# Image rows of the second 13x13 convolution in seven tiles instead of four, and the large kernels merged in the first scan

## The chip, the cores and the metric

The kernel runs on one core of a Trainium2 chip. It is one launch that computes a whole four-layer network. The metric is the time of the core on the device in microseconds (us); a lower time is better. Times of a kernel are medians of several runs. Profiles come from one profiled execution, whose own time stands beside its span.

## The reference

Input and output are x[8, 384, 32, 32] in fp32: 8 images (B), 384 channels (C), 32 x 32 pixels. Four layers follow each other:

```
layer 0: xn = rmsnorm(x);  x += res_scale * (scale_mod * (mamba(xn) + flip(mamba(flip(xn))))
                                             + sigmoid(dwconv3x3(xn)) * xn)
layer 1: conv mixer (1x1, depthwise 3x3, 1x1), linear attention, then an MLP with GELU, each residual
layer 2: out = sum over 7 depthwise kernels (13x13, 5x5, 7x7, 7x7 dil. 2, 3x3 dil. 3, 4, 5),
               each with its own batch norm
layer 3: x_pw = bn(einsum('bchw,oc->bohw', x, pw_w)) + x
         out  = gelu(bn(dwconv13x13(x_pw)) + bn(x_pw * dw1_w))
```

The mamba of layer 0 holds a recurrence over the 1024 pixels of an image, h = dA * h + dBu, for 384 channels x 16 states, once forward and once backward. As convolutions are linear, the seven kernels of layer 2 can be added up into one 13x13 kernel per channel, and the two branches of layer 3 into another.

## The kernel before

**Scans.** Image by image (8 scans, one per image), `scan(b)` runs the recurrence in 12 units (direction, half image, 128 channels) of 4 rounds. A round has two half-rounds of this kind: ScalarE makes `da` (L840), VectorE multiplies `du` (L845), runs two scan instructions (L857) and in half of the units saves a `carry` (L862), GpSimd multiplies the result `hs` by C (L866), and TensorE sums it into `acc` (L551). The inputs `dlt`, `vr` (L786) and `bct` (L772) are loaded by SP, one unit ahead. Eight `hs` tiles are in turn.

**What is woven into the scans.** `jobs` (L1189) is a list of generators with a total cost and a stretch of rounds in which each is due; after every round the loop lets the job that is furthest behind yield once. There are `fold()` (layer 1's weights scaled), `prepare` (below), `front(b)` for the next image and `layer1(b)` for the one before. Tiles called `w` (four in turn, `wtile`, L511) hold weights for all of these, and the merged kernels too. The framework then schedules the instructions: the built order of an engine can differ from that of the program's text.

**Merging the large kernels.** `kernels(small, large)`, run as the job `prepare`, makes for each of three chunks of 128 channels the merged kernel `g2` of layer 2 and `g3` of layer 3. For each: SP loads the weights (L197, L213), GpSimd clears a `w` tile (L199, L215), VectorE adds each branch scaled into it (`merge`, L184 for the first branch, L186 for the others: 21 instructions for `g2`, 4 for `g3` and one addition, L222), and GpSimd's queue stores it to DRAM (L210, L224). They are read again only at the end of the kernel.

**The two 13x13 convolutions.** After the last scan and the last `layer1`, `conv` runs with `g2` (tag a), then the 1x1 product of layer 3 (L372), then `conv` with `g3` (tag b). `conv` works on 48 tiles of 8 channels. A tile n has

- image rows `xt`: a DMA from DRAM on GpSimd's queue (L296) into 32 partitions, then two VectorE copies (`shift`, L302) that put shifted versions into the other partitions. Four `xt` tiles are in turn.
- a window set `tp`: the merged kernel laid out as bands, four DMAs, two on SP and two on ACT (L245). Twenty are in turn; 16 sets for b are asked for during the product.

Then two groups of 32 matmuls (L326) make four channels each. In b each group ends with a GELU on ScalarE (L394) and a DMA of the result on GpSimd's queue (L395). Six `ot` tiles and six PSUM tiles are in turn. In a, results are copied to `yt` (L340, L342) and stored every four groups (L344).

The order in `conv`: rows of tiles 0 and 1 are loaded, tile 0 is shifted; at the start of tile n, tile n+2 is loaded and n+1 shifted. In the built program, POOL has the loads 0 to 3, then outputs of tile 0, load 4, outputs of tiles 1 and 2, load 5, and from there on always the two outputs of tile n and then load n+3. ACT has the GELUs of tile n and the two DMAs for window set n+20 by turns, up to set 47.

Two pools hold the tiles: `cw` (three `xo` tiles, into which the product writes its rows; its weights `pwt`; `gbias`) and `cx` (`xt`, `yt`, `yp`, `tm`, `ot`). Both stay open to the end.

Of the kernel before, what the change touches and what calls it, by code (L numbers as in the profile page):

```python
# [10 lines left out]
FP = mybir.dt.float32  # L11
# [5 lines left out]
P = 128  # L17
C = 384
NC = C // P
# [21 lines left out]
N_WIN, NCH = 20, 8  # L41
# [27 lines left out]
def tile_layers(  # L69
# [31 lines left out]
    BW = B * W  # L101
# [7 lines left out]
    RL = PADW + B * (W + PADW) + 3  # L109
    x2_d = dram.tile([C, H, RL], FP, tag="x2_d", name="x2_d")  # L110
    y2_d = dram.tile([C, H, B, W], FP, tag="y2_d", name="y2_d")
    xp_d = dram.tile([C, H, RL], FP, tag="xp_d", name="xp_d")
    g2_d = dram.tile([C, NSH, TG, KT], FP, tag="g2_d", name="g2_d")
    g3_d = dram.tile([C, NSH, TG, KT], FP, tag="g3_d", name="g3_d")
# [33 lines left out]
    def bns(name, c):  # L148
        i = _BN.index(name)
        return bn_s[:, c, i : i + 1]  # L150

    def bnt(name, c):
        i = _BN.index(name)
        return bn_t[:, c, i : i + 1]
# [102 lines left out]

    NQ = C // 4
    GB = 4
    with tc.tile_pool(name="cw", bufs=1, reuse_waits="tile") as cwp, tc.tile_pool(  # L260
        name="cx", bufs=2, reuse_waits="tile"
    ) as cxp, tc.tile_pool(
        name="cps", bufs=6, space=PSUM, reuse_waits="tile"
    ) as cps:
        xos = []
        for i in range(3):
            t = cwp.tile([P, NC, 2, RL], FP, tag=f"xo{i}", name=f"xo{i}")
            nc.gpsimd.memset(t, 0.0)
            xos.append(t)
        pwt = cwp.tile([P, NC, C], FP, tag="pwt", name="pwt")  # L270
        nc.scalar.dma_start(pwt, pw_t.rearrange("(k p) o -> p k o", p=P))
        gbias = cwp.tile([P, NQ], FP, tag="gbias", name="gbias")
        for q in range(4):
            nc.scalar.dma_start(gbias[q * H : (q + 1) * H, :], biasq_d[q, :].partition_broadcast(H))
        def conv(g_d, src_d, tag, put):

            xts = {}

            def places(n):

                return [H * ((n % 2 * 2 + e) % NSH) for e in range(NSH)]

            def load(n):
                for m in range(n, min(n + 1 + N_WIN // 2, NB_C)):
                    if (tag, m) not in wins:
                        load_windows(g_d, tag, m, [nc.sync, nc.scalar])
                if n >= NB_C:
                    return  # L290
                at = places(n)
                xt = cxp.tile([P, NCH, RL], FP, tag="xt", name=f"xt_{tag}_{n}", bufs=4)
                src = bass.AP(
                    src_d.tensor, src_d[NCH * n, 0, 0].offset, [[RL, H], [H * RL, NCH], [1, RL]],
                )
                nc.gpsimd.dma_start(xt[at[0] : at[0] + H], src)  # L296
                xts[n] = xt

            def shift(n):
                at, xt = places(n), xts[n]  # L300
                for e in (1, 2):
                    nc.vector.tensor_copy(  # L302
                        xt[at[e] : at[e] + e * H, :, 0 : RL - e - (e - 1)],
                        xt[at[0] : at[0] + e * H, :, e : RL - (e - 1)],
                    )


            for n in range(2):
                load(n)
            shift(0)  # L310
            for g in range(NQ):
                n, first = divmod(4 * g, NCH)
                if first == 0:
                    load(n + 2)
                    if n + 1 < NB_C:
                        shift(n + 1)
                    xt, tp = xts.pop(n), wins[tag, n]
                ps = cps.tile([P, HALF], FP, tag="cv", name=f"cv_{tag}_{g}")
                for t in range(KT):
                    for e in range(4):  # L320
                        c = first + e
                        row = xt[:, c, NSH * t : NSH * t + B * (W + PADW) - PADW]
                        rhs = bass.AP(
                            row.tensor, row.offset, [row.ap[0], [W + PADW, B], [1, W]]
                        )
                        nc.tensor.matmul(  # L326
                            ps[H * e : H * (e + 1), 0:BW],
                            tp[:, c, :].rearrange("p (j t) -> p j t", t=KT)[:, :, t], rhs,
                            start=(t == 0), stop=(t == KT - 1), skip_group_check=True,
                        )  # L330
                put(g, ps[:, 0:BW])

        y2v = y2_d.rearrange("(g q) h b w -> g (q h) (b w)", q=4)
        hold = {}

        def put2(g, ps):
            if g % GB == 0:
                hold["t"] = cxp.tile([P, GB, BW], FP, tag="yt", name=f"yt_{g}")
            if g % 2:
                nc.scalar.copy(hold["t"][:, g % GB, :], ps)  # L340
            else:
                nc.vector.tensor_copy(hold["t"][:, g % GB, :], ps)  # L342
            if g % GB == GB - 1:
                nc.gpsimd.dma_start(y2v[g - GB + 1 : g + 1].rearrange("g p n -> p g n"), hold["t"])  # L344

        conv(g2_d, x2_d, "a", put2)


        pbias = cwp.tile([P, NC, 1], FP, tag="pbias", name="pbias")
        for m in range(NC):  # L350
            ps = cps.tile([P, HALF], FP, tag="cv", name=f"pb_{m}")
            for k in range(NC):
                nc.tensor.matmul(
                    ps[:, 0:1], pwt[:, k, m * P : (m + 1) * P], bias2[:, k, :],
                    start=(k == 0), stop=(k == NC - 1),
                )
            nc.vector.scalar_tensor_tensor(
                pbias[:, m, :], ps[:, 0:1], bns("pw", m), bnt("pw", m), ALU.mult, ALU.add
            )
            nc.vector.tensor_add(pbias[:, m, :], pbias[:, m, :], bias2[:, m, :])  # L360

        yf = y2_d.rearrange("(k p) h b w -> p k (h b w)", p=P)
        xf = xp_d.rearrange("(k p) h r -> p k h r", p=P)
        NB = 2 * BW
        for t in range(H // 2):
            yt = cxp.tile([P, NC, NB], FP, tag="yp", name=f"yp_{t}", bufs=3)
            nc.sync.dma_start(yt, yf[:, :, t * NB : (t + 1) * NB])
            xo = xos[t % 3]
            for m in range(NC):
                ps = cps.tile([P, HALF], FP, tag="cv", name=f"pw_{t}_{m}")  # L370
                for k in range(NC):
                    nc.tensor.matmul(  # L372
                        ps[:, 0:NB], pwt[:, k, m * P : (m + 1) * P], yt[:, k, :],
                        start=(k == 0), stop=(k == NC - 1),
                    )
                tm = cxp.tile([P, NB], FP, tag="tm", name=f"tm_{t}_{m}", bufs=3)
                nc.scalar.activation(  # L377
                    tm, ps[:, 0:NB], AF.Identity, bias=pbias[:, m, :], scale=bns("pw", m)
                )
                for r in range(2):  # L380
                    mid = xo[:, m, r, PADW : PADW + B * (W + PADW)].rearrange("p (b w) -> p b w", w=W + PADW)[:, :, 0:W]
                    nc.vector.tensor_add(  # L382
                        mid, tm[:, r * BW : (r + 1) * BW].rearrange("p (b w) -> p b w", w=W),
                        yt[:, m, r * BW : (r + 1) * BW].rearrange("p (b w) -> p b w", w=W),
                    )
            nc.gpsimd.dma_start(xf[:, :, 2 * t : 2 * t + 2, :], xo)
            if t < N_WIN:
                load_windows(g3_d, "b", t, [nc.scalar, nc.sync])

        ov = out.rearrange("b c h w -> (c h) b w")  # L390

        def put3(g, ps):
            ot = cxp.tile([P, BW], FP, tag="ot", name=f"ot_{g}", bufs=6)
            nc.scalar.activation(ot, ps, AF.Gelu, bias=gbias[:, g : g + 1])  # L394
            nc.gpsimd.dma_start(  # L395
                ov[g * P : (g + 1) * P], ot.rearrange("p (b w) -> p b w", w=W)
            )

        conv(g3_d, xp_d, "b", put3)


def _layers01(tc, nc, B, xv, x2_d, dram, ident, mean_w, eps5, eps6, one, half, minus1, vec, bns, bnt,
# [12 lines left out]
    with ExitStack() as ctx:  # L415
# [7 lines left out]
        def scratch(shape, name):  # L423
            return dram.tile(shape, FP, tag=name, name=name)
# [9 lines left out]
        g_d = scratch([B, C, L], "g_d")  # L434
# [494 lines left out]
        prepare = kernels(t2, lambda name: sp.tile([P, NC * C], FP, tag="w", name=name, bufs=N_W))  # L929
# [254 lines left out]
        rounds = 4 * NC * NR  # L1184
        seconds = [layer1(b) for b in range(B)]


        jobs = [[fold(), 36, 0, rounds, 0], [prepare, 7, rounds, 2 * rounds, 0]]
        for b in range(1, B):  # L1189
            jobs.append([front(b), 100, max(0, (b - 1) * rounds - 8), b * rounds - 8 - 1, 0])  # L1190
        for b in range(B - 1):
# [121 lines left out]
```

## Time and profile before

| what | us |
|---|---|
| median of 3 runs (5093.32 to 5104.8) | 5100.76 |
| the profiled execution's own time | 5049.81 |
| its span | 5048.0 |
| scan of image 0 (142.4 to 668.5) | 526.1 |
| scan of image 1 (671.9 to 1169.6) | 497.7 |
| scan of image 2 (1171.0 to 1663.8) | 492.8 |
| first 13x13 convolution, matmuls (4433 to 4645) | 212 |
| product of layer 3, matmuls (4656 to 4781) | 125 |
| second 13x13 convolution, matmuls (4795 to 5042) | 247 |

Busy over the whole span: TensorE (PE) 83%, VectorE (DVE) 75%, GpSimd (POOL) 59%, ScalarE (ACT) 52%; the mean granted TensorE clock is 0.906.

How to read it. A line of instructions names the line of the program, the engine, the operation, the tiles (out<-in), shapes and the number of instructions. In the list of groups "| busy us, mean ns | idle before us <-releasers" follow. In the timeline, start and duration stand first, and idle time before with what ended it stands in brackets. PEld are weight loads of TensorE; POOLq, SPq and ACTq the issue of an engine's instructions. A row of stretches gives: start and end, length, then busy time and number of instructions for PE, PEld, DVE, ACT and POOL, the granted clock, the share of the 16 DMA engines, and GB/s. The share can exceed 1, as packets in flight overlap.

### The profile page before, as it was taken

Reading aid. Unit: us, or ns where it says so; the run is one execution under the profiler, and the core shown is the slowest. Engines: PE = TensorE matmul, PEld = TensorE weight load, DVE = VectorE, ACT = ScalarE, POOL = GpSimd, SP = SyncE. Lnnn points to the kernel's source line nnn. Section 1 sums busy time; section 2 is a strip of 40 time slices with the busy share of each in tenths; the row PEclk is TensorE's granted clock in tenths of the full one; section 3 lists DMA queues with packets and bytes.
Section 4 is the critical chain, followed back from the end, with each engine's and each line's share of the span. In section 5 each row is a group of like instructions: output and inputs, shape, how many; then the busy total and the mean of one; then the engine's idle time right before and its main releaser. Section 6 shows DMA issues by size and latency. Waiting matters only on the chain. (4 is left out here: it accounts for less than half of the span.)

```text
span 5048.0 us, 58439 instructions
## 1 busy us (share of the span) xinstructions
PE 4205.7 (83%) x20128; PEld 1787.7 (35%) x20128; DVE 3789.3 (75%) x3861; ACT 2632.2 (52%) x3735; POOL 2975.1 (59%) x1546
## 2 busy tenths in 40 slices
PE   7555568898989998988888898988888869978877
PEld 2211113332333333333333333333333324466366
DVE  1689889988988898788978887888898821066256
ACT  3546435784577557756765676568546613100211
POOL 1467567676666676666666666666776750032156
PEclk9676779899989998999899999999898979999989
DMA  8975556577657765776567646765754581399686
GB/s 229 276 235 180 178 157 208 204 219 195 216 181 217 202 215 176 215 207 217 180 199 214 223 170 195 231 211 174 181 169 133 160 177 41 71 215 233 212 189 142
DMA packets 543121, 965.28 MB, mean 191 GB/s; under 512 B 56569, under 2 KB 220905, under 8 KB 542825
## 3 DMA queue, kind: packets, MB, share of 16 engines
q1 hardware_dynamic: 401648, 663.89, 44.2%
q0 software_dynamic: 58048, 205.76, 15.4%
q10 hardware_dynamic: 83128, 91.90, 6.4%
q8 instruction: 159, 2.61, 0.2%
q14 instruction: 138, 1.12, 0.1%
HBM read 726.36 MB, written 234.98 MB: 190 GB/s over the span
## 5 line engine op out<-in xcount | busy, mean ns | idle before, releaser
L866 POOL TENSOR_TENSOR hs<-hs,bct 128x1024 f32<-128x1024 f32 x768 | 2418.2, 3149 | 939.6 <-DVE carry L862 422.9
L840 ACT ACTIVATE da<-dlt,neg_a 128x512 f32<-128x512 f32 x1536 | 1036.7, 715 | 1055.1 <-DVE hs L857 987.9
L857 DVE TENSOR_TENSOR_SCAN hs<-da,carry,du 128x512 f32<-128x512 f32 x768 | 942.7, 1266 | 175.3 <-PE acc L551 129.8
L845 DVE TENSOR_TENSOR du<-vr,bct 128x1024 f32<-128x1024 f32 x768 | 1019.2, 1327 | 46.3 <-DMA vr<-v_d 34.9
L857 DVE TENSOR_TENSOR_SCAN hs<-da,du 128x512 f32<-128x512 f32 x768 | 900.8, 1208 | 128.6 <-PE acc L551 59.9
L551 PE MATMUL acc<-hs,selt 128*32 128x512 f32 x2304 | 546.7, 663 | 140.9 <-POOL hs L866 140.7
L533 PE MATMUL mf<-ln,w 128*128 128x512 f32 x1152 | 546.1, 620 | 22.8 <-DMA w<-w_d 11.7
L1166 PE MATMUL mo<-hm,w 128*128 128x512 f32 x1152 | 530.3, 599 | 13.8 <-DVE xx L1133 13.8
L546 PE MATMUL acc<-hs,selt 128*32 128x512 f32 x768 | 428.5, 653 | 74.4 <-POOL hs L866 63.7
L533 PEld LDWEIGHTS mf<-ln,w 128*128 128x128 f32 x1152 | 222.0, 200 | 331.7 <-issue 270.4
L533 PE MATMUL in<-xn,win 128*128 128x512 f32 x576 | 295.7, 654 | 44.0 <-DMA win<-in_inproj_t 23.6
L1166 PEld LDWEIGHTS mo<-hm,w 128*128 128x128 f32 x1152 | 214.7, 190 | 307.5 <-issue 281.2
L840 ACT ACT_TABLE_LOAD x233 | 298.9, 1283 | 9.5 <-DMA dw_i<-h_d 3.0
L326 PE MATMUL cv_b<-xt_b,tp_b 128*32 128x256 f32 x3072 | 193.6, 407 | 67.9 <-DVE xt_b L302 44.1
L302 DVE COPY xt_b<-xt_b 32x2496 f32<-32x2496 f32 x96 | 147.8, 1540 | 108.0 <-DMA xt_b<-xp_d 103.9
L326 PE MATMUL cv_a<-xt_a,tp_a 128*32 128x256 f32 x3072 | 186.0, 390 | 47.6 <-DVE xt_a L302 21.4
L1136 POOL DMA_DIRECT2D x_d<-xx x48 | 56.5, 1179 | 281.4 <-DVE xx L1133 274.1
L551 PE MATMUL dw<-dw_i,t3b 96*32 96x512 f32 x1056 | 205.6, 656 | 11.1 <-DMA dw_i<-h_d 11.0
L533 PE MATMUL op<-g,wo 128*128 128x512 f32 x288 | 156.4, 695 | 61.3 <-DMA g<-g_d 61.3
L326 PEld LDWEIGHTS cv_b<-xt_b,tp_b 128*32 128x32 f32 x3072 | 163.8, 141 | 98.0 <-issue 69.3
L533 PEld LDWEIGHTS in<-xn,win 128*128 128x128 f32 x576 | 114.1, 207 | 215.2 <-issue 161.5
L326 PEld LDWEIGHTS cv_a<-xt_a,tp_a 128*32 128x32 f32 x3072 | 159.7, 138 | 74.3 <-issue 28.7
(196 smaller groups left out, 5724.7 us busy)
## 6 DMA issues: line engine op xcount, KB each, us to landing
dlt<-dl_d SPq DMA_DIRECT2D x384, 256.0 KB, 4.6
vr<-v_d SPq DMA_DIRECT2D x384, 256.0 KB, 5.0
bct<-bc_d SPq DMA_DIRECT2D x256, 256.0 KB, 3.7
ut<-u_d SPq DMA_DIRECT2D x192, 257.5 KB, 5.5
lc_i<-xn_d SPq DMA_DIRECT2D x192, 228.8 KB, 5.4
dw_i<-h_d SPq DMA_DIRECT2D x192, 228.8 KB, 5.6
w<-w_d SPq DMA_DIRECT2D x64, 576.0 KB, 6.1
w<-in_w SPq DMA_DIRECT2D x64, 576.0 KB, 5.9
```

Of the source, the lines that this page charges most:

```text
L302: nc.vector.tensor_copy(xt[at[e] : at[e] + e * H, :, 0 : RL - e - (e - 1)], xt[at[0] : at[0] + e * H, :, e : RL - (e - 1)],)
L326: nc.tensor.matmul(ps[H * e : H * (e + 1), 0:BW], tp[:, c, :].rearrange("p (j t) -> p j t", t=KT)[:, :, t], rhs, start=(t == 0), stop=(t = ...
L533: product = nc.tensor.matmul(ps, w[:, k, m * P : (m + 1) * P], rhs[k] if isinstance(rhs, list) else rhs[:, k, :], start=(k == 0), stop=(k ...
L546: first = product()
L551: tc.keep_in_program_order(product())
L840: nc.scalar.activation(da[:, bass.ts(j, HALF)], dlt[:, bass.ts(j, HALF)], AF.Exp, scale=neg_a[:, g, r : r + 1],)
L845: nc.vector.tensor_mul(pairs(du), pairs(vt), bct[r][:, 0:1, :].to_broadcast([P, 2, HALF]),)
L857: nc.vector.tensor_tensor_scan(t[:, s][:, way], da[:, s][:, way], du[:, s][:, way], k_c if second else 0.0, ALU.mult, ALU.add,)
L866: made.append(nc.gpsimd.tensor_mul(pairs(t), pairs(t), bct[r][:, 1:2, :].to_broadcast([P, 2, HALF])))
L1136: nc.gpsimd.dma_start(x2v[m, :, h * (H // 2) : (h + 1) * (H // 2), PADW + b * (W + PADW) : PADW + b * (W + PADW) + W,], rows(o),)
L1166: nc.tensor.matmul(acc[m], wb[:, f, m * P : (m + 1) * P], hm, start=(i == 0 and f == 0), stop=(i == FF // C - 1 and f == NC - 1),)
```

## The change

The diff does two things. `conv` gets an argument `far`, how many tiles ahead the rows are loaded: 2 for a as before, 5 for b. For b, tiles n with n % 7 of 4, 5 or 6 come from a new pool `xu` of three, so that seven are in turn. This pool is opened after the pool `cw` is closed, and lies in its place; for that, `cx` is opened first, `gbias` goes to `cx`, and `yt`, `yp`, `tm` go to `cw`. Second, the stretch of the job `prepare` is rounds 0 to 48 (scan of image 0) instead of 48 to 96 (scan of image 1).

```diff
-    with tc.tile_pool(name="cw", bufs=1, reuse_waits="tile") as cwp, tc.tile_pool(
-        name="cx", bufs=2, reuse_waits="tile"
-    ) as cxp, tc.tile_pool(
+    with tc.tile_pool(name="cx", bufs=2, reuse_waits="tile") as cxp, tc.tile_pool(
         name="cps", bufs=6, space=PSUM, reuse_waits="tile"
     ) as cps:
+        gbias = cxp.tile([P, NQ], FP, tag="gbias", name="gbias", bufs=1)
+        mid_ctx = ExitStack()
+        cwp = mid_ctx.enter_context(tc.tile_pool(name="cw", bufs=1, reuse_waits="tile"))
+        more = {}
...
-        def conv(g_d, src_d, tag, put):
+        def conv(g_d, src_d, tag, put, far):
...
-                xt = cxp.tile([P, NCH, RL], FP, tag="xt", name=f"xt_{tag}_{n}", bufs=4)
+                if "pool" in more and n % 7 >= 4:
+                    xt = more["pool"].tile([P, NCH, RL], FP, tag="xu", name=f"xt_{tag}_{n}")
+                else:
+                    xt = cxp.tile([P, NCH, RL], FP, tag="xt", name=f"xt_{tag}_{n}", bufs=4)
...
-            for n in range(2):
+            for n in range(far):
                 load(n)
...
-                    load(n + 2)
+                    load(n + far)
...
-        conv(g2_d, x2_d, "a", put2)
+        conv(g2_d, x2_d, "a", put2, 2)
...
-        conv(g3_d, xp_d, "b", put3)
+        mid_ctx.close()
+        with tc.tile_pool(name="xu", bufs=3, reuse_waits="tile") as more["pool"]:
+            conv(g3_d, xp_d, "b", put3, 5)
...
-        jobs = [[fold(), 36, 0, rounds, 0], [prepare, 7, rounds, 2 * rounds, 0]]
+        jobs = [[fold(), 36, 0, rounds, 0], [prepare, 7, 0, rounds, 0]]
```

In the built program of after, POOL has the loads 0 to 5, the two outputs of tile 0, load 6, and so on: the two outputs of tile n and then load n+6. TensorE's and VectorE's order in both convolutions is unchanged. On VectorE the merges of the first `g2` stand in one block after the `du` of the sixth half-round of scan 0, ahead of image 1's normalisation; those of the second and third `g2` partly singly and partly in a block in the fourth and seventh unit, those of the three `g3` singly in the second, fifth and ninth unit. On SP the loads of some weights (`win_1_1`, `fold_1`) now wait for the store of a merged kernel, whose `w` tile they take over. Outside the scans of images 0 and 1 and the end of the kernel, the order of instructions is as before.

More of the change, by code (lines that the diff above doesn't have):

```diff
@@ L271, in tile_layers @@
         nc.scalar.dma_start(pwt, pw_t.rearrange("(k p) o -> p k o", p=P))
-        gbias = cwp.tile([P, NQ], FP, tag="gbias", name="gbias")
         for q in range(4):
             nc.scalar.dma_start(gbias[q * H : (q + 1) * H, :], biasq_d[q, :].partition_broadcast(H))
-        def conv(g_d, src_d, tag, put):
+        def conv(g_d, src_d, tag, put, far):
             xts = {}
@@ L337, in put2 @@
             if g % GB == 0:
-                hold["t"] = cxp.tile([P, GB, BW], FP, tag="yt", name=f"yt_{g}")
+                hold["t"] = cwp.tile([P, GB, BW], FP, tag="yt", name=f"yt_{g}", bufs=2)
             if g % 2:
@@ L365, in tile_layers @@
         for t in range(H // 2):
-            yt = cxp.tile([P, NC, NB], FP, tag="yp", name=f"yp_{t}", bufs=3)
+            yt = cwp.tile([P, NC, NB], FP, tag="yp", name=f"yp_{t}", bufs=3)
             nc.sync.dma_start(yt, yf[:, :, t * NB : (t + 1) * NB])
@@ L375, in tile_layers @@
                     )
-                tm = cxp.tile([P, NB], FP, tag="tm", name=f"tm_{t}_{m}", bufs=3)
+                tm = cwp.tile([P, NB], FP, tag="tm", name=f"tm_{t}_{m}", bufs=3)
                 nc.scalar.activation(
```

## The prediction

> **What bounds the kernel now.** I read the chain of work that ended last first. Its last 390 us are the product (4656 to 4781 us) and the second 13x13 convolution (4788 to 5044 us), and in the convolution it runs through POOL's DMA issues with idle "issue" stretches of 3.5 to 6 us. Then the groups of that stage:
>
> ```profile
> L326 PE MATMUL cv_b<-xt_b,tp_b 128*32 128x256 f32 x3072 | 193.6, 407 | 67.9 <-DVE xt_b L302 44.1 <-issue 12.5 <-ACT ot L394 11.3
> L395 POOL DMA_DIRECT2D out<-ot x96 | 109.5, 1141 | 98.6 <-ACT ot L394 96.3 <-DVE xt_b L302 1.3 <-issue 0.6
> L302 DVE COPY xt_b<-xt_b 32x2496 f32<-32x2496 f32 x96 | 147.8, 1540 | 108.0 <-DMA xt_b<-xp_d 103.9 <-PE cv_b L326 2.3
> L296 POOL DMA_DIRECT2D xt_b<-xp_d x48 | 48.2, 1004 | 4.7 <-DMA xp_d<-xo 4.4 <-issue 0.3
> ```
>
> TensorE waits for the shifted copies, and VectorE's copies wait 103.9 us for the image rows to land. No engine is full. The timeline shows one such stall:
>
> ```profile
> 4817.47 3.36 DVE L302 COPY xt_b<-xt_b 32x2496 f32<-32x2496 f32 x2 [5.09 <-DMA xt_b<-xp_d]
> 4818.35 1.16 POOL L296 DMA_DIRECT2D xt_b<-xp_d  x1 [0.25 <-issue]
> 4820.94 13.45 PE L326 MATMUL cv_b<-xt_b,tp_b 128*32 128x256 f32 x192 [4.61 <-DVE xt_b L302]
> 4821.35 0.23 PEld L326 LDWEIGHTS cv_b<-xt_b,tp_b 128*32 128x32 f32 x4 [0.20 <-issue]
> 4824.69 0.47 ACT L394 ACTIVATE ot<-cv_b,gbias 128x256 f32<-128x256 f32 x1 [7.78 <-DMA tp_b<-g_d]
> ```
>
> After the gap, weight loads come in fours every 0.43 us until 4826: half speed. At full speed GELUs start 1.81 us apart (4806.11, 4807.91), so a group of 32 matmuls takes 1.81 us and a tile of image rows (two groups) 3.61. The stage runs slower, in two parts: GELUs start at 4798.79 (first), 4949.90 (57th) and 5042.83 (last), which is 5.4 us a tile for the first 28 tiles and 4.65 for the other 20. The first 28 have a window set (the kernel weights of the tile 20 ahead) loading beside them. The stretches, with the first convolution ahead of them for comparison (last columns: granted clock, DMA share, GB/s):
>
> ```profile
> 4433.00:4645.00 212.00, 185.52 (x3070) 159.70 (x3072) 155.88 (x143) 17.51 (x47) 66.09 (x68) 0.98 1.07 244
> 4795.00:4950.00 155.00, 117.99 (x1792) 97.30 (x1792) 85.61 (x56) 26.16 (x56) 88.55 (x81) 0.90 0.92 192
> 4955.00:5044.00 89.00, 71.73 (x1216) 63.15 (x1216) 56.46 (x37) 18.01 (x38) 62.67 (x56) 1.00 0.58 122
> ```
>
> **What the Trainium skill says.** "SBUF — State Buffer", section "SBUF: two separate sides", says that VectorE and GpSimd share a pair of SBUF ports under an exclusive lock, and that GpSimd cannot write DMA descriptors while VectorE copies fp32 in a fast mode. The trace agrees: an output DMA's issue takes 0.89 us at the median but up to 2.16, and ends when a copy of 1.45 us ends. "TensorE: Matmul & The Clock Gate", section "What's actually happening": the array falls to half clock after some 3.4 us of idleness; the trace has it after a 4.6 us gap and not after 1.0 us. "DMA: Bandwidth & Descriptors", section "SWDGE vs HWDGE vs iDMA": each DMA engine goes round its queues in turn, so window loads can slow the row loads without starving them; the row loads' median landing is 8.0 us in the first convolution, where the engines are full, and 5.6 in the second.
>
> **The change, part by part.**
>
> **1. Row tiles, 4 to 7, loaded 5 ahead.** No instruction is added. In the built order of before, the load of tile n+3 stands on POOL behind the two outputs of tile n. The loop from the end of tile n to the start of n+3: GELU 0.5, hand-over 0.3, an output issue 0.9, load issue 1.0 (mean), landing 5.6, two copies 3.1: 11.4. With the tile's own 3.6 that is 15.0 us for three tiles, 5.0 each; the stage shows (5042.8 - 4795.1) / 48 = 5.16. In the built order of after, six loads go first and then load n+6 follows the outputs of tile n: 15.0 / 6 = 2.5 us, below TensorE's 3.61. The loop stops to bind, and with it the half-clock restarts.
>
> What is late next? (a) The port pair: two copies 2.90, held up by 0.25 each when a DMA issue slips in between (copies of 1.70 beside 1.45), and of three DMA issues per tile two fit at the copies' ends and one, about 0.65, needs a pause of VectorE: 2.90 + 0.50 + 0.65 = 4.05 us a tile, an estimate (below it 3.61 if all three find gaps, above 4.4 if a copy is awaited more often). (b) The DMA engines, where windows load. POOL's queue took 49.7% of 244 us for about 47 tiles, 2.58 a tile; the windows' two queues 15.6% + 15.2% for 28 sets, 2.68 each. Together 5.26 us of the engines per tile. The first convolution kept them at a share of 1.11: 5.26 / 1.11 = 4.74. Bounds: a tile moves as many bytes as there (313 KB rows, 256 out, 512 windows), and there took (4645.49 - 4436.96) / 47.5 = 4.39; but its windows cost more, 65.5% of 206 us / 47 = 2.87, giving 5.45 / 1.09 = 5.0. I take 4.74. Windows cannot lag far: ACT issues half of each set in its own order, ahead of GELUs, in both programs at the same tiles (in after some of these issues also wait for the matmuls that free their buffer, at most one group, 1.8, which six PSUM tiles hide).
>
> Sum: 28 x 4.74 + 20 x 4.05 = 132.7 + 81.0, plus 1.6 for the first group at half clock: 215.3 against 247.7. It saves 32 us. Two more loads at the start stand behind the first tile's on the same queue: nothing, at worst 1 us. The three extra tiles lie where the product's tiles lay; their loads must wait for the last xp_d write anyhow. The exchange of addresses moves the memsets of xo: their listed waits don't include the last x_d writes, so they stay ahead of the first convolution's loads, at nothing (at worst their 4.9 us).
>
> **2. Merging in the first scan.** It is 75 merges (12 + 12 at L184, 51 at L186), 6 memsets, 6 loads on SP, 6 stores on POOL, all moved. Where merges stand singly between scan steps, every other one waits for GpSimd's product:
>
> ```profile
> 634.47 2.31 DVE L186 SCALAR_TENSOR_TENSOR g<-kw,bn_s,g 128x10 f32<-128x10 f32 x1
> 636.69 2.44 DVE L857 TENSOR_TENSOR_SCAN hs<-da,carry,du 128x512 f32<-128x512 f32 x2
> 639.05 0.20 DVE L186 SCALAR_TENSOR_TENSOR g<-kw,bn_s,g 128x5 f32<-128x5 f32 x1
> ```
>
> so a pair costs 2.5 us; a block of 21 in a row starts one every 0.15, some 3 us. Before: the first 21 stand singly at the end of scan 0, where a unit took 43.5 us with VectorE never idle (29.0 where it does nothing else): 14.5, and two pairs beside it, 5.0. The rest is in scan 1, which took 497.7 us against 492.8 and 491.1 for the next two, 6. Removed: 25.5. After, by the built order: the first block falls in VectorE's wait of 3.55 us at 184.7, nothing if its weights are there (else up to 5, one load's landing); g3's three sets stand singly, 5 each, the first half hidden (VectorE idles 10.8 of 39.9 us there); the other two blocks cost 5.5 and 7.5, partly single. 2.5 + 5 + 5 + 5.5 + 7.5 = 25.5. Net 0, bounds -12 (half hidden) and +12. On SP the loads of weights win_1_1 and fold_1 now wait for a merged tile's store, and the scan's loads stand behind them; at 148 to 193 us SP waits for ACT anyhow, which hides the first. The loads' issues on SP (0.4 to 0.6 us each) cost nothing beside that; on POOL six memsets of 0.95 and six stores of 0.6 are 9 us in a scan where it is busy 327 of 526, nothing. A store waits for its merges with a product hs behind it, some 3 us, which the eight hs tiles cover; without that cover it would be 3 us for each of six.
>
> So 5049.8 of the profiled execution (span 5048.0) becomes 5017.8. The shown runs' median is 5100.76, 51 above the profiled one; I take the saving off it: 5069. About 0.2%, 10 us, is what a measurement can tell from no change.
>
> **Rivals.** *The DMA engines don't bind* (for: TensorE's next tile needs no window sooner than 20 tiles on; against: ACT's order). All 48 tiles at 4.05: 196, saves 51: 5050. *The loads land later as they are sooner asked for*: windows and rows fill the engines at 5.0 and POOL at 4.4: 140 + 88 + 2 = 230, saves 18; with merges at +6, 12: 5089. *Nothing measurable*: the latter with merges at +12, saves 6: 5095. *Slower*: SP stands behind a merged tile. In before the first block took 618.8 to 680.7, 62 us, until its store could go. A weight load on SP that waits for such a store holds the scan's loads behind it; what is loaded ahead is one unit, about 40 us, so each hold starves the scan by 22. Three blocks of g2, three holds: 66 on top of the forecast, 5135. It decides from 32 us of starvation on. Against it: in the built order most merges stand in blocks. Little done at all is excluded: the built order shows the six loads first.
>
> **Chances.** Forecast 0.50 (own range 5059 to 5079), DMA not binding 0.22, late landings 0.15, nothing measurable 0.06, slower 0.07. Range 5042 to 5094, which takes in savings of 59 to 7. Faster 0.87, same 0.06, slower 0.07.
>
> **What would show it.** Right: no gaps of TensorE over 3 us between 4795 and the end, weight loads never in fours after the first group; copies' wait for rows far below 104 us; DMA share 1.05 or more in the first 28 tiles and about 4.7 us a tile; POOL and VectorE limiting in the last 20 at about 4.0. Scan 0 near 526 us with merges in 184 to 490, scan 1 near 492. Wrong: tiles of 5.4 in the first part (landing grew), 4.0 throughout (DMA not binding), or scan 0 over 545 with SP waiting for stores.

## The result, and the profile after

| | us |
|---|---|
| changed kernel, median of 4 runs (5038.39 to 5054.14) | 5042.0 |
| kernel before, runs beside them (5093.32 to 5114.69) | 5102.78 |
| ratio, 95% interval | 0.9884 [0.9857, 0.9911] |
| profiled execution of the changed kernel, its span | 5038.39, 5036.6 |

The change saves some 60 us here. A second measurement of both (below) gives 0.9914 [0.9899, 0.9928], 43 us; 32 were forecast. Where they came from, by stage, in two traces of each kernel:

| stage, us | before | before, second trace | after | after, second trace |
|---|---|---|---|---|
| scans 0 and 1 together | 1027.2 | 1030.7 | 1006.6 | 1006.5 |
| scans 2 to 7 together | 2895.4 | 2939.0 | 2929.6 | 2898.9 |
| first convolution | 212.2 | 217.6 | 214.5 | 216.7 |
| second convolution | 247.6 | 257.6 | 208.7 | 210.5 |
| span | 5048.0 | 5114.2 | 5036.6 | 5008.5 |

Two stages changed: the second convolution by 37 to 49 us, the first two scans by 21 to 24. Scans 2 to 7, which the change leaves alone, differ by 44 us between two executions of the same kernel; this, not the change, is why the first pair of traces is only 11 us apart.

The groups of the second convolution (busy, mean ns, then idle and what ended it):

```profile
L330 PE MATMUL cv_b<-xt_b,tp_b 128*32 128x256 f32 x3072 | 184.5, 393 | 38.3 <-DVE xt_b L306 25.7 <-ACT ot L398 6.7 <-issue 4.3
L306 DVE COPY xt_b<-xt_b 32x2496 f32<-32x2496 f32 x96 | 149.2, 1554 | 68.0 <-DMA xt_b<-xp_d 63.4 <-PE cv_b L330 2.4
L399 POOL DMA_DIRECT2D out<-ot x96 | 135.3, 1414 | 42.8 <-ACT ot L398 30.7 <-DVE xt_b L306 9.8 <-DMA xt_b<-xp_d 1.5
L398 ACT ACTIVATE ot<-cv_b,gbias 128x256 f32<-128x256 f32 x96 | 44.9, 475 | 177.6 <-DMA tp_b<-g_d 82.3 <-DMA out<-ot 56.1 <-PE cv_b L330 37.2
```

TensorE's idle time fell from 67.9 to 38.3 us (some 14 us of either stand ahead of the first matmul) and the copies' wait for rows from 103.9 to 63.4. Two things are late now: GELUs wait 82.3 us for window DMAs, and an output's issue on GpSimd takes 1414 ns instead of 1141. The stretches (columns as before; first convolution, then the part with and the part without window loads):

```profile
4453.60:4668.10 214.50, 183.78 (x3073) 159.74 (x3074) 155.72 (x142) 17.52 (x47) 73.61 (x68) 0.99 1.09 241
4820.20:4954.90 134.70, 116.25 (x1920) 96.44 (x1920) 93.35 (x61) 25.84 (x56) 95.69 (x81) 0.96 1.07 228
4955.00:5029.00 74.00, 68.13 (x1152) 59.20 (x1152) 52.73 (x34) 18.58 (x41) 73.74 (x55) 1.00 0.69 141
```

In the first part the DMA share is now 1.07, near the first convolution's 1.09; it was 0.92 before. In the second part POOL is busy 73.74 us of 74.00. At the border between them stands this, on ACT:

```profile
4950.88 0.47 ACT L398 ACTIVATE ot<-cv_b,gbias 128x256 f32<-128x256 f32 x1 [4.38 <-DMA tp_b<-g_d]
4954.08 0.31 ACTq L245 DMA_DIRECT2D tp_b<-g_d  x1
4954.49 1.94 ACT L398 ACTIVATE ot<-cv_b,gbias 128x256 f32<-128x256 f32 x5 [3.13 <-DMA tp_b<-g_d]
```

As soon as ACT has issued its last window DMA, five GELUs run in a row: their matmuls had been done, and they only stood behind that DMA in ACT's order. So in the change GELUs lag behind TensorE while windows load: four to six finished groups stand in the six PSUM tiles, one in before. TensorE's last matmul of tile 28 ends 124.2 us after the stage's start, the GELU of that group only starts at 134.7.

In scans 0 and 1 VectorE does the same work in both kernels, and waits less. First before, then after, scan 0 and scan 1 (third pair of numbers: VectorE):

```profile
142.40:668.50 526.10, 296.18 (x1052) 92.84 (x1048) 453.62 (x429) 264.07 (x372) 327.02 (x162) 0.69 0.64 204
671.90:1169.60 497.70, 432.25 (x1664) 164.08 (x1666) 434.47 (x480) 319.12 (x441) 337.85 (x159) 0.92 0.66 203
```

```profile
147.20:667.20 520.00, 299.44 (x1074) 95.95 (x1072) 469.37 (x491) 274.04 (x381) 330.80 (x171) 0.71 0.68 216
668.60:1153.70 485.10, 427.61 (x1642) 161.11 (x1644) 423.39 (x418) 314.13 (x436) 331.71 (x148) 0.92 0.66 199
```

VectorE's 888.1 us became 892.8, but its time without work fell from 135.7 to 112.3. Scan 0 took 15.7 us more of VectorE's work and became 6 shorter.

### The profile page after: what moved, and what is told of

The parts are those of the page before. It is cut to its first block, busy times and chain, and to the rows that moved or that the text cites. A ratio compares the mean times of both kernels' runs of the same rounds, so it can differ in the third digit from the quotient of the medians.

```text
span 5036.6 us, 58480 instructions
## 1 busy us (share of the span) xinstructions
PE 4203.6 (83%) x20128; PEld 1781.9 (35%) x20128; DVE 3791.7 (75%) x3861; ACT 2637.3 (52%) x3738; POOL 2997.3 (60%) x1546
## 5 line engine op out<-in xcount | busy, mean ns | idle before, releaser
L851 DVE TENSOR_TENSOR du<-vr,bct 128x1024 f32<-128x1024 f32 x768 | 1033.0, 1345 | 31.4 <-DMA vr<-v_d 19.6
L557 PE MATMUL acc<-hs,selt 128*32 128x512 f32 x2304 | 541.5, 660 | 134.8 <-POOL hs L872 134.7
L552 PE MATMUL acc<-hs,selt 128*32 128x512 f32 x768 | 420.9, 643 | 58.6 <-POOL hs L872 50.3
L539 PEld LDWEIGHTS mf<-ln,w 128*128 128x128 f32 x1152 | 222.8, 200 | 339.4 <-issue 271.9
L1172 PEld LDWEIGHTS mo<-hm,w 128*128 128x128 f32 x1152 | 214.5, 190 | 309.1 <-issue 281.3
L330 PE MATMUL cv_b<-xt_b,tp_b 128*32 128x256 f32 x3072 | 184.5, 393 | 38.3 <-DVE xt_b L306 25.7
L306 DVE COPY xt_b<-xt_b 32x2496 f32<-32x2496 f32 x96 | 149.2, 1554 | 68.0 <-DMA xt_b<-xp_d 63.4
```

The lines of the kernel that those rows point to most:

```text
L306: nc.vector.tensor_copy(xt[at[e] : at[e] + e * H, :, 0 : RL - e - (e - 1)], xt[at[0] : at[0] + e * H, :, e : RL - (e - 1)],)
L330: nc.tensor.matmul(ps[H * e : H * (e + 1), 0:BW], tp[:, c, :].rearrange("p (j t) -> p j t", t=KT)[:, :, t], rhs, start=(t == 0), stop=(t = ...
L539: product = nc.tensor.matmul(ps, w[:, k, m * P : (m + 1) * P], rhs[k] if isinstance(rhs, list) else rhs[:, k, :], start=(k == 0), stop=(k ...
L552: first = product()
L557: tc.keep_in_program_order(product())
L851: nc.vector.tensor_mul(pairs(du), pairs(vt), bct[r][:, 0:1, :].to_broadcast([P, 2, HALF]),)
```

## The experiments

The kernel before took 5106 us (median) beside the first four kernels and 5055 and 5054 beside the other eight, so a ratio is always against the runs beside it. Stage times are from one trace each. "First part" is the second convolution's time up to the start of the 56th GELU, the last of the first 28 tiles (4949.9 in the trace of before, where the prediction calls it the 57th), divided by 28; "last part" is the rest, divided by 20. Where GELUs lag, this border lies later than TensorE's own; where that matters, the parts by the end of TensorE's tile 28 are given beside it.

### Is the difference in the later scans the change's?

The kernel before, unchanged.

> The kernel before, profiled a second time. Theory A (scans 2 to 7, whose instructions the change leaves alone, run at a speed that varies from execution to execution; the first profile of before caught a fast one): the span is 5085 to 5105 us, scans 2 to 7 take 2920 to 2945 us together instead of 2895, scans 0 and 1 about 1028 to 1035, the second convolution 247. Rival B (the change slows scans 2 to 7 by some 40 us, by another placement of tiles): the span stays near 5050 and scans 2 to 7 near 2895 us.

Measured: span 5114.2, scans 2 to 7 2939.0 us, the second convolution 257.6. Theory A holds for the scans, so nothing in the unchanged ones is to be explained. Its span and its 247 us for the second convolution were missed by some 10 us, so a stage, too, differs by that much between two executions of one kernel.

### The two edits apart

Rows only (the changed kernel with the old stretch of `prepare`):

```diff
-        jobs = [[fold(), 36, 0, rounds, 0], [prepare, 7, 0, rounds, 0]]
+        jobs = [[fold(), 36, 0, rounds, 0], [prepare, 7, rounds, 2 * rounds, 0]]
```

> The seven row tiles and the load 5 ahead alone, merges left in the second scan. Theory A (as the two traces show: rows -39 us, the moved merges -20 us): 39 us below before, ratio 0.9924, and 20 us above the changed kernel. Rival B (the prediction's own sizes, merges net 0): the whole gain, 60 us, ratio 0.988. Rival C (the prediction's 32 us for rows with its two bounds): ratio 0.9937. In all, the second convolution takes 207 to 211 us.

Merges only (the kernel before with the new stretch):

```diff
-        jobs = [[fold(), 36, 0, rounds, 0], [prepare, 7, rounds, 2 * rounds, 0]]
+        jobs = [[fold(), 36, 0, rounds, 0], [prepare, 7, 0, rounds, 0]]
```

> The merges in the first scan alone, the convolution as before. Theory A: 20 us below before, ratio 0.996; scan 0 near 520 us and scan 1 near 485 in the profile, the second convolution 247. Rival B (the prediction's net 0, -12 to +12): ratio 1.000, from 0.9976 to 1.0024. If the two single edits sum to more or less than the 60 us of both, they meet somewhere.

And both, the changed kernel once more:

> The changed kernel once more, beside the two single edits. Single edits so far: rows 0.9949 (-26 us), merges 0.9975 (-13 us), together -39. Theory A (the two edits do not meet; their sum holds): ratio 0.992, from 0.990 to 0.9945. Rival B (they help each other, as the first result of -60 us says): ratio 0.988.

| kernel | ratio, 95% interval | scans 0 + 1 | second convolution |
|---|---|---|---|
| rows only | 0.9949 [0.9928, 0.9969] | 1031.2 | 210.3 |
| merges only | 0.9975 [0.9966, 0.9984] | 1008.6 | 246.1 |
| both, again | 0.9914 [0.9899, 0.9928] | 1006.5 | 210.5 |

By the traces each edit acts on its own stage alone, and both help. By the times, rows give 26 us and merges 13; the sum, 39, agrees with the 43 of both: theory A of the third run. The forecast of net 0 for the merges, with its gains up to 12, misses the 13 narrowly, and more clearly the 22 that the trace of that run has in the scans. For rows only, theory A's 0.9924 lies just outside the interval, and rival C's 0.9937 inside it: its stage is 37 to 47 us shorter in the trace, the time only 26. In the profiled execution of rows only the stretch between the last scan and the first convolution took 379.3 us (365 to 373 in the other thirteen traces) and the first convolution 222.8. This is not one execution's scatter: all six runs of rows only lie at 5070 to 5088, those of the next kernel, whose second convolution is as long, at 5045 to 5066. The changed kernel has the same pools and shows nothing of the kind (369 us and 214 to 217). What it comes from is open. Single kernels can thus be some 10 us out by the times, beyond their intervals, and what an edit is worth is better read from its stage. The merges' 13 us, too, are not seen again in the times of the next pair (0.9912 with the old merges, 0.9923 with the new), while scans 0 and 1 are again 20 us shorter in its traces (1030.0 and 1009.6).

### More tiles, or an earlier place in the queue?

```diff
-        def conv(g_d, src_d, tag, put):
+        def conv(g_d, src_d, tag, put, far):
...
-        conv(g2_d, x2_d, "a", put2)
+        conv(g2_d, x2_d, "a", put2, 2)
...
-        conv(g3_d, xp_d, "b", put3)
+        conv(g3_d, xp_d, "b", put3, 3)
```

Four tiles as before, no new pool; only `far` is 3 in b, with the old merges and then, in a second kernel, with the new ones.

> No tile added: still four row tiles, but the second convolution loads rows 3 tiles ahead instead of 2; merges left in the second scan. It keeps the half of the row edit that moves a load on POOL's queue (load n+4 behind the outputs of tile n) and leaves out the tiles. Theory A (the loop of 15.0 us from the end of tile n to the start of the loaded one is what binds, so it is 15.0 / 4 = 3.75 us a tile here, below the 4.76 that the DMA engines give in the first part and at TensorE's 3.61 in the second): 28 x 4.8 + 20 x 3.9 = 212 us for the stage, 35 us below before, ratio 0.993, within 5 us of the rows edit alone. Rival B (the number of tiles decides: a load finds no free tile earlier than before): stage near 247, ratio 1.000.

> The version that the runs so far point to: four row tiles as before, loaded 3 ahead, and the merges in the first scan. Theory A (the place of the load on POOL's queue is the whole of the row edit): second convolution 207 to 211 us, ratio within 0.003 of the changed kernel's. Rival B (three more tiles are worth something of their own): 5 us or more above the changed kernel.

| kernel | ratio, 95% interval | second convolution | first, last part by GELUs | by TensorE |
|---|---|---|---|---|
| `far` 3, four tiles, old merges | 0.9912 [0.9888, 0.9936] | 209.4 | 4.53, 4.13 | 4.53, 4.13 |
| `far` 3, four tiles, new merges | 0.9923 [0.9905, 0.9941] | 213.5 | 4.57, 4.28 | 4.55, 4.31 |
| the change (again) | 0.9914 [0.9899, 0.9928] | 210.5 | 4.86, 3.73 | 4.53, 4.18 |

One digit does what the three tiles, the new pool and the change of addresses do: with the load of tile n+4 instead of n+3 behind the outputs of tile n, the loop of 15.0 us is spread over four tiles, 3.75 each, and no longer binds. What binds then looks like the change again (`far` 3 with old merges, the two parts): a DMA share of 1.05 in the first, POOL busy 78.01 of 81.30 us in the last.

```profile
4847.00:4975.00 128.00, 109.44 (x1813) 94.28 (x1817) 87.44 (x57) 25.55 (x56) 97.31 (x83) 0.97 1.05 231
4975.00:5056.30 81.30, 73.51 (x1264) 65.23 (x1256) 59.25 (x38) 18.38 (x39) 78.01 (x57) 1.00 0.70 147
```

By GELUs the change seems to lose 0.3 us a tile in the first part and to win 0.4 to 0.5 in the last. By TensorE there is no such difference: the GELUs lag, and catch up when the last window DMA is out. Nor do seven tiles lay up a stock: when tile 28 is done, no copied tile is ready in any of the three, and the rows of only one more have landed. The built order of ACT differs as well: in the change one GELU and one window DMA by turns from the seventh tile on, with four tiles mostly two and two as in before; whether this makes the GELUs lag is not shown. The rival of the second run, 5 us or more for three more tiles, is met by the medians (5015.1 against 5009.7) and lies within the intervals. If the tiles are worth anything, it is not more than these few us.

### What binds each part now?

First the window loads are left out, then moved, then the outputs are moved:

```diff
                     if (tag, m) not in wins:
+                        if tag == "b" and m >= N_WIN:
+                            wins[tag, m] = wins[tag, m - N_WIN]
+                            continue
                         load_windows(g_d, tag, m, [nc.sync, nc.scalar])
```

> The changed kernel; window sets 20 to 47 of the second convolution are not loaded, those of 20 tiles before are used again (left out: the right weights of 28 tiles). Theory A (the DMA engines bind the first 28 tiles at 4.7 us each): without 2.68 us of engine time per tile they run at 3.7, the last 20 unchanged at 3.8 to 4.0; stage 28 x 3.75 + 20 x 3.85 = 182 us, 27 us below the changed kernel. Rival B (port pair or hand-overs bind near 4.05 as the prediction has it): 28 x 4.1 + 20 x 3.85 = 192, 17 below. Rival C (neither): no change, 209.

```diff
-                        load_windows(g_d, tag, m, [nc.sync, nc.scalar])
+                        load_windows(g_d, tag, m, [nc.sync] if tag == "b" else [nc.sync, nc.scalar])
```

> The changed kernel; all four DMAs of a window set of the second convolution are issued by SP, none by ACT, so that GELUs do not stand behind them. Theory A (it is the engines' work, rows, results and windows together, that binds the first 28 tiles): 4.6 to 4.8 us a tile as before, stage 205 to 212, no change in time. Rival B (ACT's order binds, a GELU waits behind an issue that waits for a free buffer; windows may lag by up to 20 tiles): first 28 tiles at 3.8 to 4.1 us, stage 185 to 192, 20 us below the changed kernel.

```diff
-            nc.gpsimd.dma_start(
+            nc.sync.dma_start(
                 ov[g * P : (g + 1) * P], ot.rearrange("p (b w) -> p b w", w=W)
```

> As no_window_loads (28 sets not loaded, others used again; left out: their right weights), and the results of the second convolution are stored by SP instead of GpSimd, two of three DMA issues per tile fewer on GpSimd. Theory A (the 4.04 us a tile of that run are GpSimd's three issues, held up by VectorE's copies through the shared ports): without them TensorE's 3.61 bind, stage 48 x 3.65 + 2 = 177 us, 19 us below no_window_loads. Rival B (the copies and the hand-over of rows bind): 4.0 us a tile stay, stage near 195.

And, of the second, the form with [nc.sync] for both convolutions:

> As windows_by_sync, and the window sets that the first convolution loads are issued by SP alone too, so that ACT's copies to yt do not stand behind them. Theory A (the same order binds there): the first convolution falls from 215 to 222 us to about 200, and the whole to a ratio of 0.985. Rival B (there the DMA engines have work for the whole stage, 28 sets of a and most of 20 of b, so that a free ACT only moves the wait): first convolution 212 to 222 us, ratio 0.9887 as windows_by_sync.

| kernel | ratio, 95% interval | second convolution | first part | last part |
|---|---|---|---|---|
| the change (again) | 0.9914 [0.9899, 0.9928] | 210.5 | 4.86 | 3.73 |
| 28 window sets not loaded | 0.9899 [0.9877, 0.9921] | 195.7 | 4.08 | 4.07 |
| windows of b by SP | 0.9887 [0.9870, 0.9903] | 194.1 | 4.02 | 4.08 |
| windows of both by SP | 0.9862 [0.9843, 0.9882] | 192.8 | 4.09 | 3.92 |
| not loaded, outputs by SP | 0.9842 [0.9816, 0.9868] | 176.4 | 3.72 | 3.61 |

Three limits lie one under the other. Without the loads the first part falls to 4.08, not to 3.75: rival B, the price of the port pair. But the loads need not be left out: issued by SP, they cost nothing that the stage shows either (rival B, with a stage of 194 where I had 185 to 192). So a full set of DMA engines did not bind the tiles by itself. What ACT waits for between 4795 and 4925 us in the changed kernel (second trace):

```profile
ACT ot L398 <- DMA tp_b<-g_d: 92.3, 39, 7.6
ACT ot L398 <- PE cv_b L330: 10.6, 7, 2.1
```

and with the windows on SP:

```profile
ACT ot L398 <- DMA out<-ot: 76.5, 47, 3.8
ACT ot L398 <- PE cv_b L330: 23.8, 16, 3.2
```

In the built program a window DMA waits for a counter that the DMA eight before it, two sets earlier, has to set by landing. The second trace has the landing for 30 of the 56 window DMAs that ACT issues in this stage, and 24 of them start within half a us of it. The Trainium skill ("DMA: Bandwidth & Descriptors", section "Anatomy of one DMA — SWDGE (gpsimd) path") says where such a wait is spent: the DMA engines never wait on semaphores, the engine that issues does, before it dispatches. It says so of DMAs issued by GpSimd; the 92 us here (82 in the whole stage of the first trace) show it for ACT. Landing takes 8.4 us at the median when the engines are full, and a GELU behind that DMA on ACT waits along: two sets per 8.4 us is 4.2 us a set, an estimate, to which issues and hand-overs come. A late GELU reaches TensorE in two ways that the first trace shows: PSUM tiles stay full (TensorE waits 6.7 us for GELUs), and GpSimd's queue, in which the row loads stand behind the outputs, waits 30.7 us for GELUs. On SP nobody stands behind the window DMA. The landing grows to 11.0 us there, and the sets come in later than the tiles advance: the DMA share is 1.07 to 1.11 from 4814 to 4934, some 36 tiles into the stage, where in the change the loads end with tile 28. Twenty sets in turn allow that.

The next limit is GpSimd. With windows on SP its queue has no gap:

```profile
4869.58 1.44 POOL L300 DMA_DIRECT2D xt_b<-xp_d  x1
4871.01 2.70 POOL L399 DMA_DIRECT2D out<-ot  x2
4873.70 1.44 POOL L300 DMA_DIRECT2D xt_b<-xp_d  x1
4875.13 2.70 POOL L399 DMA_DIRECT2D out<-ot  x2
```

A load and two outputs take 1.44 + 2.70 = 4.14 us, the tile. An output's issue alone is shorter: 0.89 us at its shortest, which was its median in before; here the median is 1.74. With the outputs on SP, and the window loads left out, the tile takes 3.61 to 3.72; in these stretches of that run (first and last part) TensorE is busy 102.45 of 102.50 and 73.98 of 74.00 us, POOL 25.55 and 11.81:

```profile
4784.00:4886.50 102.50, 102.45 (x1775) 85.69 (x1776) 91.01 (x63) 25.75 (x55) 25.55 (x27) 0.97 0.86 161
4886.50:4960.50 74.00, 73.98 (x1304) 65.75 (x1296) 45.62 (x32) 19.33 (x41) 11.81 (x14) 1.00 0.77 140
```

That is TensorE's own pace, the third limit. The edit also takes the row loads out from behind the outputs; that GpSimd's queue was full without it (81.10 of 81.10 us in the last part with windows on SP, 82.30 of 82.30 with none loaded) speaks for the issues. The GELUs' wait for stored results, the 76.5 us above, is no limit of its own: an output lands after 7.3 us with windows on SP and after 4.2 with none loaded, at the same pace. Moving the first convolution's windows too brings nothing that its stage shows (213.2 us against 212 to 224 elsewhere), as rival B says. The ratio, 0.9862, is nearer to theory A's 0.985 than to 0.9887; as the first convolution did not become shorter, I put that down to other kernels beside it, and it is not tested further. Both versions with windows on SP compute everything and beat the change, the one of b by 15 us beside it (4994.2 against 5009.7).

### What do the merges cost in each place?

In both kernels the same three statements are taken out:

```diff
-                merge(g, src, k, d, bns(f"l2_{j}", c), j == 0)
...
-            merge(g, src, KS, 1, bns("dwk", c), True)
...
-            nc.vector.tensor_add(mid, mid, dlt[:, c, :])
```

> The kernel before without VectorE's merges and the three additions that belong to them; loads, clearing and stores of the merged tiles stay (left out: the merged kernels of layers 2 and 3 remain zero). Its scans 0 and 1 give what the merges cost in the kernel before, where they take 1027 to 1031 us together. Prediction: 25.5 us, so 1003. Theory A (the second scan gives 15 us back, not 6, as a comparison of scan 1 with later scans missed): 29 to 32 us, so 998, with scan 1 near 485. Rival B (loads and stores of the merged tiles, not the merges, are what costs): under 20 us.

> The changed kernel without VectorE's merges and the three additions (left out as in the run before). Its scans 0 and 1 take 1006.5 us with the merges. Prediction: the merges cost 25.5 us in the first scan, so 981. Theory A (half of what was priced hides in VectorE's waits): they cost 8 to 13 us, so 994 to 998. Rival B (they cost about what they cost before, and the gain is of another kind): 977.

There is one run of each kernel without merges, beside the second traces of before and after:

| scans 0 + 1, us | length | VectorE busy | VectorE without work |
|---|---|---|---|
| before (second trace) | 1030.7 | 892.0 | 138.7 |
| before without merges | 984.0 | 865.8 | 118.2 |
| after (second trace) | 1006.5 | 891.3 | 115.2 |
| after without merges | 1002.6 | 855.9 | 146.7 |

The numbers are beyond both forecasts: the merges cost 43 to 47 us in before and 4 in after. In before they add 26 us of work and 20 of waiting; in after they add 35 of work, of which 31 fall into waits that are there without them. Taking out merges changes the built order of other instructions too (loads on SP from the second unit on, some `du` and `hs` of the tenth), and the two kernels without merges differ by 18.6 us; so these totals are not clean. In before without merges the second, third and ninth unit, which hold none in before, are 2 to 7 us shorter as well; and why the after kernel without merges waits longer is open.

Single units are cleaner. Counted through scans 0 and 1, three that lost merges became shorter by 13.7 (twelfth: 46.9 to 33.2), 8 to 9 (fifteenth) and 7 us (sixteenth), and are then as long as in before without merges (33.1, 36.4 and 37.1 in after, 33.1, 36.5 and 37.0 there). So the merges had cost 29 us in these three. Units 1 to 11 of scan 0, which hold the merges in the change, became only 5.5 to 6 us longer in sum (5.8 and 5.5 in the two pairs of traces): the fifth to seventh by 4 to 5.5 each, the fourth, with the block of the second `g2`, by nothing; the second and third are taken up below.

## Why the prediction was right and where it was short

**The number.** 5069 was forecast, with a range of 5042 to 5094. The measured 5042.0 lies on the lower edge of that range, outside the forecast's own 5059 to 5079, and nearest to the 5050 of a rival (DMA engines that don't bind) which is not what happened. That it fell inside is partly luck; the second measurement's 43 us, taken off the same 5100.76, would be 5058.

**The loop of 15.0 us on GpSimd's queue: right, and shown.** The load's place, not the number of tiles, gave the stage's gain. In the changed kernel TensorE has one gap over 3 us after the stage's start (two in the second trace), where before had eight, and 104 matmuls of over 0.5 us instead of 282. "No gap" was said, so that is nearly, not fully, as forecast.

**4.74 us a tile for 28 tiles: the number fits the GELUs, and the owner was wrong.** 28 x 4.74 + 1.6 = 134.3 were forecast and 134.7 measured at the GELUs. TensorE takes 124.2 us for these tiles (126.9 in the second trace), so as TensorE's pace the term is 7 to 10 us too large. The price came from the engines' share in the first convolution, which has the same order on ACT. The runs show that full engines set the landing time, and ACT's order turns landing time into the tile's pace; the prediction had named the order ("Windows cannot lag far: ACT issues half of each set in its own order"), but put the wait in it down to matmuls that free a buffer, at most one group and hidden. It is a wait for an earlier window's landing, 82 us in all. So the rival in which the engines don't bind describes not the change but a kernel one edit away: its 196 us for the stage is the 194.1 of the windows on SP.

**4.05 us a tile for the last 20: nearly right, and GpSimd's alone.** With the windows left out or issued by SP the stage takes 4.08 and 4.04 us a tile, as worked out. In the change TensorE's last 20 tiles take 84.5 and 83.6 us in the two traces against 81.0, so this term is 3 us too small; counted at the GELUs they take 74.0, because some had only been kept waiting. GpSimd makes 55 issues there in 73.74 us, 1.34 each, 4.0 for the three of a tile. The forecast had built the 4.05 from VectorE's time and held both engines to be limiting; VectorE is busy 52.73 us of 74.00, so it is GpSimd's queue that is full.

**Merges at net 0: the step that failed.** "Removed 25.5 ... added 25.5" was out on both sides. Removed: scan 1 was set against the next two scans (492.8 and 491.1) to find 6 us. But scan 1 without merges takes 485.1 to 485.3 (after, and before with the merges taken out), so its neighbours, at 491 to 503, were no baseline; the term was 13 to 16. Added: half of one `g3` set and the first `g2` block were put into VectorE's waits, and 25.5 us remained. Units 1 to 11 show 5.5 to 6, with at most the 5 us to add of the two pairs that left their end; by the runs without merges, as far as they separate it, 31 of 35 us of work fall into waits. The first trace had the figure to warn of this: VectorE was idle 72.5 of 526.1 us in scan 0. Of the 28 us by which the first measurement exceeds the forecast of 32, the stage gives 6.6 (215.3 forecast, 208.7 measured) and the two scans 21, by the traces. The second measurement, 43 us, leaves 11 to explain, which is less than the 29 that its traces have for both.

**Rivals.** SP behind a merged tile's store, the slower case: the wait exists, and once only, 11.2 us instead of the 62 of its price (SP in scan 0 of after; total, times, longest):

```profile
SPq L517 <- DMA g_d<-g: 11.2, 1, 11.2
```

The largest stall that the merges bring was not among the rivals. The load of the first `g3`'s weights is issued at 227.1, after SP has waited 10.5 us for the landing of a `vr`, and lands some 14 us later; VectorE stands in front of its first merge:

```profile
241.22 0.27 DVE L184 TENSOR_SCALAR g<-k,bn_s 128x52 f32<-128x52 f32 x1 [18.00 <-DMA k<-in_dwk]
```

It costs nothing net that can be seen: the second and third unit take 83.6 us together, against 82.0 and 86.9 in the two traces of before, where VectorE spends 22 us of the 82.0 in other waits. The addresses' exchange, the memsets of `xo` and the two additional loads at the start brought nothing that can be seen.

**The base.** Taking the saving off the runs' median, 5100.76, and not off the profiled execution's 5049.81 was right: the second trace of before has 5114.2.

**A reading of the trace.** The prediction says that a long issue on GpSimd's queue ends when a copy ends; it ends 0.48 us later (last section).

## What to carry to other kernels

Ask first where a load stands in its queue, and only then how many buffers it has: here one place earlier with the old buffers gave the stage's whole gain. Here an engine that computes and issues DMAs passed the waits of its DMAs on to its results; put loads that may be late on a queue behind which nobody stands. Work moved to another stage costs only what does not fit into the waits there: take the baseline from a kernel without it, not from a neighbour that looks alike. And before a stage is split in two, see whether the engine at which the border is read lags behind the one that does the work.

## What the runs showed of the hardware

An output's issue on GpSimd's queue took 0.89 us at the median in before and 1.34 to 1.74 in the kernels that fill VectorE with copies; in "windows of b by SP" these issues and the loads' alone fill the queue. It is the copies that lengthen it. In all the traces, an output's issue that no copy overlaps takes 0.89 to 0.90 us (393 of them) and a row load's at most 0.61 (270). Beside a copy an output's takes up to 2.18, and of the 556 over 1.5 us all but two end 0.47 to 0.50 us after the end of a copy. One of them in before, with the copy that starts after it and ends at 4827.07:

```profile
4825.47 2.09 POOL L395 DMA_DIRECT2D out<-ot  x1 [5.97 <-ACT ot L394]
4825.62 1.45 DVE L302 COPY xt_b<-xt_b 32x2496 f32<-32x2496 f32 x1 [0.54 <-DMA xt_b<-xp_d]
```

Copies suffer less: their median is 1.54 us and their longest 1.92 with windows on SP, 1.45 and 1.58 with the outputs on SP and no window loads. This agrees with the lock of which the Trainium skill tells ("SBUF — State Buffer", section "SBUF: two separate sides"), and here it is GpSimd that pays most of it. Its advice, to issue from ACT or SP instead, is worth (195.7 - 176.4) / 48 = 0.40 us a tile on SP (the two runs without window loads). What makes the same scans take 2895 us in one execution and 2939 in another, at the same instructions, is open.
